# Attention block on one core: the first steps in another order (filler products, weight scaling, sums, maxima)

## The chip, the cores and the metric

One Trainium2 chip, one of its cores. The metric is device microseconds of one execution. A core has five engines that run side by side, each working through its own instructions in order: TensorE (PE in the profile; its weight loads are PEld), VectorE (DVE), ScalarE (ACT), GpSimd (POOL) and SyncE (SP), which here only issues transfers. They wait for one another through semaphores.

## What is computed

A residual attention layer: 64 batches of 128 tokens, 512 features, 16 heads of 64, one key and one value head shared by all (with a null key in front), a bias per head, a causal mask and a mask of keys.

```python
xn = layernorm(x, g_in)
q = (xn @ Wq).reshape(b, n, H, DH).transpose(0, 2, 1, 3) * scale
kv = xn @ Wkv
k, v = (kv[..., :DH], kv[..., DH:])          # the null key and value are put in front
sim = jnp.einsum('bhid,bjd->bhij', q, k) + bias
sim = where(causal or masked, -max, sim)
attn = jax.nn.softmax(sim, axis=-1)
out = jnp.einsum('bhij,bjd->bhid', attn, v)
out = layernorm(out @ Wo, g_out)
return x + out
```

All in float32.

## The kernel before

The kernel is one program whose order is written out by hand: `step(n)` runs for n from -6 to 62 and issues, for several batches at different stages, the pieces of work one after the other. Each engine gets its share of the pieces in just this order. Batches are taken in groups of four (a group g has 512 tokens).

**Tokens.** `norm_stats(m)` takes mean and variance of x_m on DVE and raises the variance to -1/2 on POOL (L246). `norm_apply(m)` scales: on DVE for the first four (L253), later a small product on DVE (nmr, L258) and then ACT (L259). Where one step has two m, both statistics are issued before either scaling. `norm_T(m)` transposes x_m with PE (pxT, L268) and copies it to xT with ACT (L269). From batch 8 on, DVE transposes (L278) and transfers move it.

**Projections.** For group 0, `q_plain` makes eight chunks of q from the weights wq (pq, L373; each has four products, over rows 2, 0, 3, 1 of wq) and ACT copies them to qT (L380). For later groups the same result comes from seven products instead of eight, per pair of halves (`product`, L422; `keep`, ACT L433; `q_out`, DVE L443 or ACT L440). They need sums of weights, s1, s2, s4 (`weight_sums`, DVE L385 to L387) and s3 (`weight_sum_3`, POOL L390, written over the part of wq that only group 0 reads), and four sums of tokens per group (`token_sum`, POOL L404). `kv_mm` (pkv, L308) makes keys, values and the null key's scores in one product; `kv_out` takes it out of PSUM on DVE (ktok L320, vs L324).

**Weights at the start.** g_in is multiplied into the rows of wq by `weights_q` (DVE L844 or ACT L848) and into wkv by DVE (L872). `weights_kv_prod` multiplies wq by the null key on POOL (L864), and DVE sums that (nq, L876) into 16 further columns of wkv (L857). `causal(u)` fills the upper triangle of the bias on POOL (L199); the second half of the bias is loaded after `causal(1)`, since it overwrites rows that this one touches.

**Softmax.** `bias_add` puts bias and mask into a tile S (POOL L466), `null_copy` the null scores (POOL L475), `scores` is PE (ps, L495) and DVE (add, L508), `scores_max` DVE (L513), `exps` ACT, one row at a time with its sum (L522), `rinv` DVE (L539), `scale` POOL (L543). Each is done for hf 0 (64 keys) and hf 1 (128 keys). The probabilities of batches 0 and 1 are transposed on PE (`attn_T_pe`, L610 and L615), those of later ones on DVE (L575) and moved by transfers (L601) into aTb, which starts as zeros.

**Values and output.** `values` and `values_end` multiply by the values (po, L636). Between the halves stands a tiny copy of DVE, `done` (L668), for order; ACT takes the result to oT (L680). Batch 0 goes through `out_mm` (py, L697) and `out_stats`; later ones in pairs with seven products (L750).

**Filler.** `keep_busy(k)` issues k products of the unit matrix with itself that nobody reads (L1191). A product of float32 leaves two records in the trace.

**Transfers.** SP issues nearly all of them in program order, and one queue works them off. Each of its eight semaphores is used in turn, so a transfer also waits until the one eight places ahead of it has landed. `load_second`, `load_late` (wo, gob) and `loads_late` issue the input of the front.

PSUM tiles with the tag "w" have two buffers, which transposes, pkv, pk, po and py share in turn.

Of the kernel before, what the change touches and what calls it, by code (L numbers as in the profile page):

```python
# [8 lines left out]
FP = mybir.dt.float32  # L9
U8 = mybir.dt.uint8  # L10
AF = mybir.ActivationFunctionType
ALU = mybir.AluOpType
# [5 lines left out]
def kernel(  # L18
# [59 lines left out]
    nc = tc.nc  # L78
# [60 lines left out]
    def load_mask(g):  # L139
        m8s[g] = gp.tile([P, TOK], U8, tag="m8", name=f"m8_{g}")  # L140
        nc.sync.dma_start(
            out=m8s[g],
            in_=mask[g * GB : (g + 1) * GB].rearrange("b n -> (b n)").partition_broadcast(P),
        )
# [28 lines left out]
    )  # L173

    def load_second():
        nc.sync.dma_start(out=nbh, in_=null_bias.partition_broadcast(P))
        nc.sync.dma_start(out=nvb, in_=cond[1].partition_broadcast(P))
        load_mask(0)
        for m in (4, 5, 6):
            load_x(m)  # L180
        load_bias(1)
        for r in range(2):
            nc.sync.dma_start(
                out=nv2[r * DH : (r + 1) * DH, :], in_=cond[1].unsqueeze(1)
            )

    def load_bias(u):
        rows = slice(u * DH, (u + 1) * DH)
        bias_r = attn_bias.rearrange("(u f r) i j -> u r i f j", u=2, r=2)[u]
        for r in range(2):  # L190
            rf = slice(r * NF, (r + 1) * NF)
            nc.sync.dma_start(out=biasp[rows, rf, 0:NL], in_=bias_r[r, 0:DH, :, 0:NL])
            nc.sync.dma_start(out=biasp[rows, rf, NL:], in_=bias_r[r, DH:N])
# [193 lines left out]
        nc.vector.tensor_tensor(s4, a12, s2, ALU.subtract)  # L387

    def weight_sum_3():
        nc.gpsimd.tensor_tensor(s3, a11, a21, ALU.subtract)  # L390

    def token_sum(g, k):

        xS[g, k] = gp.tile([P, GB // 2, HK, N], FP, tag=f"xS{k}", name=f"xS{k}_{g}", bufs=1)
        lo, hi = xT[g][:, 0 : GB // 2], xT[g][:, GB // 2 :]
        b11, b12 = lo[:, :, lo_k], hi[:, :, lo_k]
        b21, b22 = lo[:, :, hi_k], hi[:, :, hi_k]
        p, m = {
            1: (b12, b11),
            2: (b22, xS.get((g, 1))),  # L400
            3: (b22, b12),
            4: (b21, xS.get((g, 2))),
        }[k]
        nc.gpsimd.tensor_tensor(xS[g, k], p, m, ALU.subtract)  # L404
# [55 lines left out]
    def bias_add(b):  # L460
        g, t = divmod(b, GB)
        if b in (B3 + 1, B3 + 4):
            S[b] = gp.tile([P, R8, ROW], FP, tag="xT", name=f"s_{b}")
        else:
            S[b] = sp.tile([P, R8, ROW], FP, tag="s", name=f"s_{b}")
        nc.gpsimd.tensor_tensor(  # L466
            S[b][:, :, 1 : ROW - 1],
            biasp,
            mneg[g][:, t].unsqueeze(1).broadcast_to([P, R8, NL + N]),
            ALU.add,  # L470
        )

    def null_copy(b):
        g, t = divmod(b, GB)
        nc.gpsimd.tensor_copy(  # L475
            S[b][:, :, 0 : ROW : ROW - 1],
            nv[g][:, t, DH:].rearrange("p (k e) -> p e k", k=2),
        )
# [38 lines left out]
    def exps(b, hf, lo=0, hi=R8):  # L517
        if hf == 0 and lo == 0:
            rsum[b] = small.tile([P, 2, R8], FP, tag="rsum", name=f"rsum_{b}")
        for k in range(lo, hi):  # L520
            row = S[b][:, k, WITH_NULL[hf]]
            nc.scalar.activation(  # L522
                row,
                row,
                AF.Exp,
                bias=nmax[b][:, hf, k : k + 1],
                accum_out=rsum[b][:, hf, k : k + 1],
            )
# [257 lines left out]
    def pair_pow(b):  # L786
        nc.gpsimd.tensor_tensor(yn[b][1], yn[b][1], nhalf, ALU.pow)
# [23 lines left out]
    def out_stats(b):  # L811
        st = small.tile([P, 6], FP, tag="st", name=f"sto_{b}")
        nc.vector.bn_stats(st, ys[b])
        mv = small.tile([P, 2], FP, tag="mvo", name=f"mvo_{b}")
        nc.vector.bn_aggr(mv, st)
        rstd = small.tile([P, 1], FP, tag="rstdo", name=f"rstdo_{b}")
        nc.vector.tensor_scalar(rstd, mv[:, 1:2], EPS, None, ALU.add)
        nc.gpsimd.tensor_tensor(rstd, rstd, nhalf, ALU.pow)
        y = hp.tile([P, DIM], FP, tag="y", name=f"y_{b}", bufs=3)
        nc.vector.scalar_tensor_tensor(  # L820
            y, ys.pop(b), mv[:, 0:1], gob, ALU.subtract, ALU.mult
        )
        if b == B - 1:

            nc.vector.scalar_tensor_tensor(y, y, rstd, res.pop(b), ALU.mult, ALU.add)
        else:
            yr[b] = y, rstd
        ys[b] = y
# [11 lines left out]


    def weights_q(kc):
        if kc < 2:
            nc.vector.tensor_scalar(  # L844
                wq[:, kc, :], wq[:, kc, :], gin8[:, kc : kc + 1], None, ALU.mult
            )
        else:
            nc.scalar.activation(  # L848
                wq[:, kc, :], wq[:, kc, :], AF.Copy, scale=gin8[:, kc : kc + 1]
            )  # L850
# [9 lines left out]
            )  # L860

    def weights_kv_prod(kc):
        prods[kc] = sp.tile([P, H, DH], FP, tag="s", name=f"prod_{kc}")
        nc.gpsimd.tensor_tensor(  # L864
            prods[kc],
            wq[:, kc, :].rearrange("p (h d) -> p h d", d=DH),
            nkb.unsqueeze(1).broadcast_to([P, H, DH]),
            ALU.mult,
        )
# [9 lines left out]
    def step(n):  # L879
        def ok(b, end=B):  # L880
            return 0 <= b < end
# [33 lines left out]
            null_copy(nb)  # L915
        if third:
            pair_pow(p4)
        for m in mns:
            norm_stats(m)
        if fast and f == 0 and fill:  # L920
            for k in range(1, 5):
                token_sum(qg, k)
            if n == -2:
                weight_sum_3()
        if n == -4:
            bias_add(0)
            bias_add(1)
# [7 lines left out]
        if one:  # L935

            out_mm(n - 1, 0, NF if n > B3 + 1 else NC)
            if n == 1:
                attn_T_pe(1)
                bias_add(nb)  # L940
                null_copy(nb)
                out_stats(0)
        if fast:
            if f == 0:
                q_tile(qg)
# [5 lines left out]
            scores_max(B3 + 1, 0)  # L951
        if last:
            product(last_g, last_f, 4, ps_q, "a", start=False)
        if soft:
            exps(eb, 0, 0, 4)
        if third:
            out_part(p4 + 1, 0, "X")
# [10 lines left out]
        if 2 * GB <= mb < B:  # L968
            tokens_T(mb)
            if (mb + 1) % GB == 0:  # L970
                tokens_out(mb // GB)
        if soft:
            exps(eb, 0, 4)
        if soft and n != B3 + 1:
            rinv(eb, 0)
            scale(eb, 0)
        if third:
# [21 lines left out]
            product(qg, f, 2, ps_w, "w")  # L999
        elif q and not fast:  # L1000
            q_plain(qg, 2 * f)
        if soft:
            exps(eb, 1, 0, 2)
        if third and n != B3:
            pair_norm(p4)
# [19 lines left out]
        elif first:  # L1025
            out_keep("X", "yp1", "p1")
            out_product(p12, 2, ps_w, "w")
            out_part(p12, 0, "w", "yp1")
        if soft:
            exps(eb, 1, 2, 4)  # L1030
        if soft and not second:
            exps(eb, 1, 4, 6)
# [34 lines left out]
                mask_neg(qg)  # L1067
            out_part(p5673, 1, "Y", "yu2")
        if ok(n + 1) and fill:
            exps(n + 1, 1)  # L1070
        if one and n == 1:
            residual(0)
        if n == B3 - 1:
# [2 lines left out]
        if sc and n != B3:  # L1076
            scores(nb, 0)
            scores_add(nb, 0)
            if ok(n + 1) and fill:
                rinv(n + 1, 1)  # L1080
                scale(n + 1, 1)
        split = sc and n != B3
        if n == B3:
            pair_nmr(p4 + 1)
        if ok(n):
            values(n, split)
        if third and n != B3:
            pair_residual(p4 + 1)
            store(p4 + 1)
# [4 lines left out]
        if not ok(n) and fast:  # L1094
            product(qg, f, 6, ps_q, "a", start=False)
            keep("a", "u2")
        if ok(n) and not split:
            values_end(n, split)
            if n > B3 + 1:
                out_mm(n - 1, NF)  # L1100
# [6 lines left out]
            store(p4 + 1)  # L1107
            scores_max(nb, 0)

        late = first and fast  # L1110
        if sc:
            scores(nb, 1)
            scores_add(nb, 1)
# [63 lines left out]
        if n == B2 - 2:  # L1177
            second_aTb()
        if n == -4:
            for m in range(GB - 1):  # L1180
                kv_out(m, kv_mm(m))
                if m:
                    kT_out(m - 1, k_T(m - 1))
# [10 lines left out]
    nc.vector.tensor_scalar(gin8, gin, DH**-0.5, None, ALU.mult)  # L1194
    norm_stats(0)
    norm_stats(1)
    norm_apply(0)
    norm_T(0)
    norm_stats(2)
    norm_apply(1)  # L1200
    norm_T(1)
    norm_stats(3)
    norm_apply(2)
    norm_T(2)
    keep_busy(8)
    norm_apply(3)
    norm_T(3)
    keep_busy(10)
    load_second()
    weights_q(2)  # L1210
    weights_q(0)
    weights_q(3)
    weights_q(1)
    nc.gpsimd.memset(aTb, 0.0)
    for kc in range(2):
        weights_kv_prod(kc)
    nc.vector.tensor_scalar(vnb[:, 0:DH], nvb, -1.0, None, ALU.mult)
    null_order(vnb[:, DH:], nbh)
    causal(1)
    load_bias(0)  # L1220
    for n in range(-6, B - 1):
        step(n)
        if n == -6:
            for kc in range(2):
                weights_kv(kc)
            for kc in range(2, KC):
                weights_kv_prod(kc)
            load_late()
        if n == -5:
            for kc in range(2, KC):  # L1230
                weights_kv(kc)
            causal(0)
            mask_neg(0)
            weight_sums()

    load_res(B - 1)
    store(B - 3)
# [47 lines left out]
```

## Time and profile before

| | us |
|---|---|
| three runs | 1125.67, 1126.27, 1128.89 |
| median | 1126.27 |
| profiled execution, time | 1131.23 |
| its span, first to last instruction | 1129.4 |
| PE busy | 1089.5 (96%) |
| DVE busy | 808.0 (72%) |
| POOL busy | 745.3 (66%) |
| ACT busy | 678.1 (60%) |
| matmul pa L422, mean of one record | 0.38 |

The profiled execution is one of its own and stands 5 us above the median. "Busy" is time in which an engine has an instruction in it; since products overlap, a busy PE isn't one at its peak. Times inside the execution count from the span's start. A row of the timeline gives start and length, the engine, the line, what is written and read with its shape, and in brackets the idle time of the engine before it with whatever ended that.

The kernel runs in three stretches: the front up to about 130 us, a long even part, and an end of some 30 us.

### The profile page before, as it was taken

The page shows a single profiled execution, that of the slowest core. Times are in us where ns is not written, and L with a number is a line of the kernel's source. Part 1 is how long each engine was busy: PE and PEld are TensorE (multiplying, and loading weights), DVE is VectorE, ACT ScalarE, POOL GpSimd, SP SyncE. Part 2 cuts the span into 40 slices and gives each one's busy share as a digit, 9 for nine tenths or more (in the row PEclk, how much of TensorE's full clock was granted, in tenths as well). Part 3 has the DMA queues.
Part 4 walks back from the last instruction along what each step waited for, and adds up shares of the span by engine and source line. Part 5 has one row for each costly group of instructions (what it writes and reads, how often), then busy time and mean ns, then how long its engine had stood idle before and what let it go on. Part 6 is the DMA issues. An engine that isn't in the chain of part 4 may idle for free.

```text
span 1129.4 us, 27505 instructions
## 1 busy us (share of the span) xinstructions
PE 1089.5 (96%) x9780; PEld 873.0 (77%) x9780; DVE 808.0 (72%) x1741; ACT 678.1 (60%) x2710; POOL 745.3 (66%) x588
## 2 busy tenths in 40 slices
PE   6988999999999999999999999999999999999987
PEld 4565788888888888788888888888888888888643
DVE  6564677777787777678777768877777886666852
ACT  2345656666765666676565667566566756657651
POOL 5454877767675776767577676757768575777832
PEclk9999999999999999999999999999999999999999
DMA  6313244363454436345343533534353353422333
GB/s 186 121 33 96 63 128 115 93 168 98 128 131 127 118 91 169 98 124 133 122 123 91 165 105 120 132 120 118 100 163 104 125 134 99 114 75 76 96 104 101
DMA packets 107864, 130.09 MB, mean 115 GB/s; under 512 B 29264, under 2 KB 72528, under 8 KB 105936
## 3 DMA queue, kind: packets, MB, share of 16 engines
q1 hardware_dynamic: 106480, 126.96, 40.0%
q8 instruction: 78, 1.28, 0.5%
q10 hardware_dynamic: 1248, 1.38, 0.4%
q14 instruction: 58, 0.48, 0.1%
HBM read 54.86 MB, written 31.46 MB: 76 GB/s over the span
## 4 chain that ended last, share of the span: by engine, by line
PE 68%; DMA 8%; POOL 7%; DVE 6%; SPq 5%; issue 3%; ACT 3%; POOLq 0%; ACTq 0%; DVEq 0%
PE pa L422 14%; PE pyX L750 13%; PE pc L422 7%; PE ps L495 7%; PE po L636 6%; PE pyY L750 6%; DMA x<-in_x_dram 6%; PE pk L308 4%; SPq L601 4%; PE pw L422 3%; PE pyw L750 3%; PE py L697 3%; ACT s L522 2%; POOL s L543 1%; POOL xS L404 1%
## 5 line engine op out<-in xcount | busy, mean ns | idle before, releaser
L522 ACT ACTIVATE s<-s,nmax 128x65 f32<-128x65 f32 (+1 forms) x1024 | 372.2, 368 | 0.4
L466 POOL TENSOR_TENSOR s<-biasp,mneg 128x1536 f32<-128x1536 f32 x64 | 221.1, 3455 | 110.0 <-DVE sb L575 99.0
L543 POOL TENSOR_TENSOR s<-s,rinv 128x512 f32<-128x512 f32 (+1 forms) x128 | 189.2, 1479 | 119.5 <-DVE nmro L794 86.8
L680 ACT ACTIVATE oT<-po,nv 128x512 f32<-128x512 f32 x128 | 81.0, 683 | 203.2 <-PE po L636 203.2
L522 ACT ACTIVATION_READ_ACCUMULATOR s<-s,nmax 128x1 f32 x1024 | 195.2, 191 | 0.0
L750 PE MATMUL pyX<-wT,oT 128*128 128x256 f32 x696 | 164.7, 379 | 0.5 <-DVE kyu L762 0.5
L750 PEld LDWEIGHTS pyX<-wT,oT 128*128 128x128 f32 x696 | 131.9, 190 | 19.4 <-DVE kyu L762 0.9
L508 DVE TENSOR_TENSOR s<-ps,s 128x512 f32<-128x512 f32 (+1 forms) x128 | 121.6, 950 | 14.2 <-PE ps L495 13.3
L495 PEld LDWEIGHTS ps<-kT,qT 64*64 64x64 f32 x4096 | 92.2, 134 | 46.8 <-DVE s L508 24.9
L422 PE MATMUL pa<-xS,wq 128*128 128x256 f32 x480 | 123.7, 380 | 2.0 <-POOL wq L390 1.0
L513 DVE TENSOR_REDUCE nmax<-s 128x8 f32<-128x520 f32 (+1 forms) x128 | 120.2, 939 | 5.1 <-POOL s L475 3.7
L495 PE MATMUL ps<-kT,qT 64*64 64x64 f32 (+1 forms) x4096 | 116.6, 251 | 3.3 <-DVE s L508 2.6
L575 DVE STREAM_TRANSPOSE sb<-s 128x1536 f32<-128x1536 f32 x62 | 110.0, 1774 | 11.6 <-POOL s L543 4.6
L636 PE MATMUL po<-aTb,vs 64*64 64x256 f32 (+1 forms) x1240 | 114.2, 380 | 2.2 <-DVE done L668 2.2
L433 ACT COPY ku<-pa 128x256 f32<-128x256 f32 x120 | 44.7, 372 | 94.4 <-PE pa L422 94.4
L422 PEld LDWEIGHTS pa<-xS,wq 128*128 128x128 f32 x480 | 86.7, 190 | 12.2 <-ACT ku L433 1.6
L308 PE MATMUL pk<-wkv,xT 128*128 128x144 f32 x488 | 70.2, 287 | 0.0
L422 PE MATMUL pc<-xS,wS 128*128 128x256 f32 x240 | 63.2, 386 | 6.9 <-POOL xS L404 6.9
L422 PE MATMUL pa<-xS,wS 128*128 128x256 f32 x240 | 68.8, 409 | 0.0
L443 DVE TENSOR_TENSOR qT<-pw,kp 128x256 f32<-128x256 f32 x60 | 25.4, 424 | 59.8 <-ACT kp L433 59.7
L636 PEld LDWEIGHTS po<-aTb,vs 64*64 64x64 f32 (+1 forms) x1240 | 55.9, 134 | 12.2 <-issue 3.8
L246 POOL TENSOR_TENSOR rstd<-rstd,nhalf 128x1 f32<-128x1 f32 x64 | 35.8, 559 | 44.5 <-DVE rstd L245 44.4
(120 smaller groups left out, 2105.9 us busy)
## 6 DMA issues: line engine op xcount, KB each, us to landing
aTb<-sb SPq DMA_DIRECT2D x369, 64.0 KB
x<-in_x_dram SPq DMA_DIRECT2D x64, 256.0 KB
res<-in_x_dram SPq DMA_DIRECT2D x64, 256.0 KB
out_dram<-y SPq DMA_DIRECT2D x64, 256.0 KB
aTb<-sb SPq DMA_DIRECT2D x492, 32.0 KB
xd<-xb SPq DMA_DIRECT2D x14, 1024.0 KB
xT<-xd SPq DMA_DIRECT2D x56, 256.0 KB
wo<-in_L_cond_Wo_dram SPq DMA_DIRECT2D x1, 2048.0 KB
```

Of the source, the lines that this page charges most:

```text
L308: nc.tensor.matmul(pkv, xT[g][:, t, kc, :], wkv[:, kc, :], start=(kc == 0), stop=(kc == KC - 1),)
L422: nc.tensor.matmul(prod[tag], w[:, kc, f * P : (f + 1) * P], t[:, :, kc, :], start=(start and kc == 0), stop=(kc == HK - 1), skip_group_ch ...
L466: nc.gpsimd.tensor_tensor(S[b][:, :, 1 : ROW - 1], biasp, mneg[g][:, t].unsqueeze(1).broadcast_to([P, R8, NL + N]), ALU.add,)
L495: nc.tensor.matmul(pv[u * DH : (u + 1) * DH, r, f, :], qT[g][rows, f, t, hf, u], kT[b][rows, 0:nk], start=True, stop=True,)
L508: nc.vector.tensor_tensor(sv, pss.pop((b, hf)), sv, ALU.add)
L513: nc.vector.tensor_reduce(nmax[b][:, hf], S[b][:, :, WITH_NULL[hf]], AX.X, ALU.max, negate=True)
L522: nc.scalar.activation(row, row, AF.Exp, bias=nmax[b][:, hf, k : k + 1], accum_out=rsum[b][:, hf, k : k + 1],)
L543: nc.gpsimd.tensor_tensor(sv, sv, rinvs.pop((b, hf)).unsqueeze(2).broadcast_to([P, R8, sv.shape[2]]), ALU.mult,)
L575: nc.vector.transpose(sb.rearrange("p j e q -> p e j q"), S[b][:, :, 1 : ROW - 1].rearrange("p e (j k) -> p e j k", k=Q),)
L636: nc.tensor.matmul(pos[b][u][r * DH : (r + 1) * DH, half], vals[keys, b % GB, 0:DH], aT_of(b)[keys, slots, r * NF : (r + 1) * NF], start=s ...
L680: nc.scalar.activation(oT[b][:, u * NF : (u + 1) * NF, :].rearrange("p f (s q) -> p s f q", q=Q), po[u].rearrange("p h i f q -> p (h i) f q"),
L750: nc.tensor.matmul(prod[key], h[:, c, :], w[:, c, :], start=(start and c == 0), stop=(c == HC - 1), skip_group_check=not start,)
```

## The change

It edits the front only.

- The unread products: before, eight between the third and the fourth transposes and ten after the fourth; after, 5, 4, 2, 2 and 3, ahead of, between and behind the four.
- wq: rows 0 and 1 on DVE, 2 and 3 on ACT before; rows 2, 0 and 3 on DVE and only row 1 on ACT after.
- `weights_kv_prod`: the four come one after the other on POOL, in four tiles instead of two in turn, with the power of x_4 after the first; the fill of the bias comes after them.
- The memset of aTb moves from the start into step -4, the null value's preparation (vnb) from the start to the end of step -5.
- In SP's order x_4 to x_6 and the first half of the bias come before the mask and the null values; the second half of the bias is issued after mask 1 and x_7.
- `weight_sums` moves from the end of step -5 to step -4, ahead of the evacuation of pkv. `weight_sum_3` goes from POOL to DVE and, with the token sums, ahead of the statistics of its step.
- The maxima of hf 1 in the steps below 0 come after `q_out`.
- Step -1: two exponentials of hf 1, then a copy (ku), then the other six. Step 0: the reciprocals and the scaling of batch 1 come after `values`. Step 1: all exponentials of hf 0, their scaling and four of hf 1 come ahead of the bias addition and of `out_stats`.

```diff
--- before.py
+++ after.py
@@ -173,12 +173,12 @@
     )

     def load_second():
-        nc.sync.dma_start(out=nbh, in_=null_bias.partition_broadcast(P))
-        nc.sync.dma_start(out=nvb, in_=cond[1].partition_broadcast(P))
-        load_mask(0)
         for m in (4, 5, 6):
             load_x(m)
         load_bias(1)
+        load_mask(0)
+        nc.sync.dma_start(out=nbh, in_=null_bias.partition_broadcast(P))
+        nc.sync.dma_start(out=nvb, in_=cond[1].partition_broadcast(P))
         for r in range(2):
             nc.sync.dma_start(
                 out=nv2[r * DH : (r + 1) * DH, :], in_=cond[1].unsqueeze(1)
@@ -387,7 +387,7 @@
         nc.vector.tensor_tensor(s4, a12, s2, ALU.subtract)

     def weight_sum_3():
-        nc.gpsimd.tensor_tensor(s3, a11, a21, ALU.subtract)
+        nc.vector.tensor_tensor(s3, a11, a21, ALU.subtract)

     def token_sum(g, k):

@@ -840,7 +840,7 @@


     def weights_q(kc):
-        if kc < 2:
+        if kc != 1:
             nc.vector.tensor_scalar(
                 wq[:, kc, :], wq[:, kc, :], gin8[:, kc : kc + 1], None, ALU.mult
             )
@@ -860,7 +860,10 @@
             )

     def weights_kv_prod(kc):
-        prods[kc] = sp.tile([P, H, DH], FP, tag="s", name=f"prod_{kc}")
+
+        pool, tag = ((sp, "s"), (sp, "s"), (hp, "sb"), (hp, "xb"))[kc]
+        bufs = None if kc < 2 else 1
+        prods[kc] = pool.tile([P, H, DH], FP, tag=tag, name=f"prod_{kc}", bufs=bufs)
         nc.gpsimd.tensor_tensor(
             prods[kc],
             wq[:, kc, :].rearrange("p (h d) -> p h d", d=DH),
@@ -915,13 +918,13 @@
             null_copy(nb)
         if third:
             pair_pow(p4)
+        if fast and f == 0 and fill:
+            if n == -2:
+                weight_sum_3()
+            for k in range(1, 5):
+                token_sum(qg, k)
         for m in mns:
             norm_stats(m)
-        if fast and f == 0 and fill:
-            for k in range(1, 5):
-                token_sum(qg, k)
-            if n == -2:
-                weight_sum_3()
         if n == -4:
             bias_add(0)
             bias_add(1)
@@ -937,9 +940,6 @@
             out_mm(n - 1, 0, NF if n > B3 + 1 else NC)
             if n == 1:
                 attn_T_pe(1)
-                bias_add(nb)
-                null_copy(nb)
-                out_stats(0)
         if fast:
             if f == 0:
                 q_tile(qg)
@@ -951,7 +951,15 @@
             scores_max(B3 + 1, 0)
         if last:
             product(last_g, last_f, 4, ps_q, "a", start=False)
-        if soft:
+        if n == 1:
+            exps(eb, 0)
+            rinv(eb, 0)
+            scale(eb, 0)
+            exps(eb, 1, 0, 4)
+            bias_add(nb)
+            null_copy(nb)
+            out_stats(0)
+        elif soft:
             exps(eb, 0, 0, 4)
         if third:
             out_part(p4 + 1, 0, "X")
@@ -969,9 +977,9 @@
             tokens_T(mb)
             if (mb + 1) % GB == 0:
                 tokens_out(mb // GB)
-        if soft:
+        if soft and n != 1:
             exps(eb, 0, 4)
-        if soft and n != B3 + 1:
+        if soft and n not in (1, B3 + 1):
             rinv(eb, 0)
             scale(eb, 0)
         if third:
@@ -999,7 +1007,7 @@
             product(qg, f, 2, ps_w, "w")
         elif q and not fast:
             q_plain(qg, 2 * f)
-        if soft:
+        if soft and n != 1:
             exps(eb, 1, 0, 2)
         if third and n != B3:
             pair_norm(p4)
@@ -1026,7 +1034,7 @@
             out_keep("X", "yp1", "p1")
             out_product(p12, 2, ps_w, "w")
             out_part(p12, 0, "w", "yp1")
-        if soft:
+        if soft and n != 1:
             exps(eb, 1, 2, 4)
         if soft and not second:
             exps(eb, 1, 4, 6)
@@ -1067,7 +1075,7 @@
                 mask_neg(qg)
             out_part(p5673, 1, "Y", "yu2")
         if ok(n + 1) and fill:
-            exps(n + 1, 1)
+            exps(n + 1, 1, 0, R8 if n == 0 else 2)
         if one and n == 1:
             residual(0)
         if n == B3 - 1:
@@ -1076,14 +1084,14 @@
         if sc and n != B3:
             scores(nb, 0)
             scores_add(nb, 0)
-            if ok(n + 1) and fill:
-                rinv(n + 1, 1)
-                scale(n + 1, 1)
         split = sc and n != B3
         if n == B3:
             pair_nmr(p4 + 1)
         if ok(n):
             values(n, split)
+        if n == 0:
+            rinv(1, 1)
+            scale(1, 1)
         if third and n != B3:
             pair_residual(p4 + 1)
             store(p4 + 1)
@@ -1094,6 +1102,10 @@
         if not ok(n) and fast:
             product(qg, f, 6, ps_q, "a", start=False)
             keep("a", "u2")
+        if n == -1:
+            exps(0, 1, 2)
+            rinv(0, 1)
+            scale(0, 1)
         if ok(n) and not split:
             values_end(n, split)
             if n > B3 + 1:
@@ -1107,7 +1119,7 @@
             store(p4 + 1)
             scores_max(nb, 0)

-        late = first and fast
+        late = fast and (first or n < 0)
         if sc:
             scores(nb, 1)
             scores_add(nb, 1)
@@ -1177,6 +1189,7 @@
         if n == B2 - 2:
             second_aTb()
         if n == -4:
+            weight_sums()
             for m in range(GB - 1):
                 kv_out(m, kv_mm(m))
                 if m:
@@ -1194,44 +1207,46 @@
     nc.vector.tensor_scalar(gin8, gin, DH**-0.5, None, ALU.mult)
     norm_stats(0)
     norm_stats(1)
+    keep_busy(5)
     norm_apply(0)
     norm_T(0)
     norm_stats(2)
+    keep_busy(4)
     norm_apply(1)
     norm_T(1)
     norm_stats(3)
+    keep_busy(2)
     norm_apply(2)
     norm_T(2)
-    keep_busy(8)
+    keep_busy(2)
     norm_apply(3)
     norm_T(3)
-    keep_busy(10)
+    keep_busy(3)
     load_second()
     weights_q(2)
     weights_q(0)
     weights_q(3)
     weights_q(1)
-    nc.gpsimd.memset(aTb, 0.0)
-    for kc in range(2):
-        weights_kv_prod(kc)
-    nc.vector.tensor_scalar(vnb[:, 0:DH], nvb, -1.0, None, ALU.mult)
-    null_order(vnb[:, DH:], nbh)
-    causal(1)
-    load_bias(0)
+    weights_kv_prod(0)
     for n in range(-6, B - 1):
         step(n)
         if n == -6:
+            for kc in range(1, KC):
+                weights_kv_prod(kc)
+            causal(1)
+            load_bias(0)
             for kc in range(2):
                 weights_kv(kc)
-            for kc in range(2, KC):
-                weights_kv_prod(kc)
             load_late()
         if n == -5:
             for kc in range(2, KC):
                 weights_kv(kc)
             causal(0)
             mask_neg(0)
-            weight_sums()
+            nc.vector.tensor_scalar(vnb[:, 0:DH], nvb, -1.0, None, ALU.mult)
+            null_order(vnb[:, DH:], nbh)
+        if n == -4:
+            nc.gpsimd.memset(aTb, 0.0)

     load_res(B - 1)
     store(B - 3)
```

## The prediction

> **What bounds the kernel.** I read the page first (span 1129.4 us, TensorE busy 96%, granted clock 0.9 or more in all 40 slices), then a table of busy time by stage, then the timeline of the first 130 us. In the stages below the columns are: stage, length, busy us of PE, PEld, DVE, ACT and POOL with their counts, granted clock, DMA share, GB/s.
>
> ```profile
> 0.00:10.00 10.00, 1.30 (x5) 0.90 (x6) 4.21 (x13) 2.07 (x3) 4.01 (x11) 1.00 0.74 269
> 10.00:20.00 10.00, 9.37 (x51) 8.34 (x51) 8.02 (x11) 3.84 (x5) 7.40 (x5) 1.00 0.71 201
> ...
> 40.00:50.00 10.00, 7.41 (x35) 5.76 (x35) 4.26 (x18) 2.99 (x6) 7.89 (x4) 0.83 0.08 26
> 50.00:60.00 10.00, 8.72 (x34) 5.09 (x32) 4.59 (x16) 4.13 (x9) 2.27 (x4) 1.00 0.22 54
> 60.00:70.00 10.00, 7.95 (x93) 6.07 (x93) 3.77 (x5) 1.71 (x5) 6.78 (x6) 1.00 0.12 42
> ...
> 110.00:120.00 10.00, 7.66 (x109) 5.12 (x101) 6.31 (x10) 7.34 (x29) 6.18 (x4) 1.00 0.05 14
> 120.00:130.00 10.00, 8.44 (x74) 6.97 (x78) 4.62 (x17) 6.77 (x32) 8.49 (x7) 1.00 0.30 84
> ...
> 200.00:1100.00 900.00, 890.17 (x8252) 732.43 (x8251) 673.23 (x1442) 574.57 (x2340) 615.12 (x480) 1.00 0.42 117
> ```
>
> From 130 us on PE is 99% busy and nothing there is edited, so whatever the front gains or loses by then arrives whole at the end. Up to 130 us PE idles 8.7 us before 10, and 13 us between 40 and 130. In 10 to 20 part of the "busy" is filler: the unread products. The timeline names the waits (start, length, engine, line, instruction; in brackets the idle time before it and what ended it):
>
> ```profile
> 11.86 1.58 DVE L253 TENSOR_SCALAR x<-x,mv,rstd 128x512 f32<-128x512 f32 x1 [0.44 <-POOL rstd L246]
> ...
> 18.77 7.03 PE L373 MATMUL pq<-xT,wq 128*128 128x512 f32 x16
> ...
> 42.60 0.66 PE L268 MATMUL pxT<-ident,x 128*128 128x128 f32 x4 [2.18 <-ACT x L259]
> ...
> 60.65 1.13 PE L422 MATMUL pc<-xS,wS 128*128 128x256 f32 x4 [1.93 <-POOL xS L404]
> ...
> 66.76 1.13 PE L422 MATMUL pa<-xS,wq 128*128 128x256 f32 x4 [1.01 <-POOL wq L390]
> ...
> 91.20 0.96 PE L636 MATMUL po<-aTb,vs 64*64 64x256 f32 x8 [2.17 <-DVE done L668]
> ...
> 112.53 0.43 PE L636 MATMUL po<-aTb,nv 64*64 64x256 f32 x2 [1.64 <-DVE qT L443]
> ```
>
> The first shows a second fact: the same normalisation took 0.54 us three times and 1.58 us here, while POOL's memset of aTb ran from 11.77 to 13.15. DVE was shut out until POOL had finished.
>
> **Start of the projections: -4.1 us.** Before, 16 records (eight unread products) run from 12.44 to 16.06 and hold back the fourth transposes, whose x was ready at 13.44; the copy to xT ends at 17.32, ACT scales wq rows 2 and 3 at 1.14 each, ten more products run, and pq starts at 18.77. After, the memset is gone from this place, so x_3 is ready at 12.4. Two products (4 records of 3.62/16 = 0.23) stand before its transposes: third transposes end 12.3, products 13.2, transposes (0.85 while slow, as at 15.86) 14.0, ACT's copy (0.58) 14.6, three products beside it. DVE scales rows 2, 0, 3 in 0.74 each from 12.4 to 14.6; ACT's row 1 (1.14) is done at 15.8 and needed only as the fourth product, at 14.6 + 3 x 0.87. So pq starts at about 14.6 (14.0 to 15.2).
>
> **The products for the null key: +1.2.** POOL now does prod 0 (2.8, as the first before), the power (0.55), then prods 1, 2, 3 (2.35 each) and only then the causal fill (0.66 + 1.09): 13.9 to about 26.4, against 22.83 before. DVE's small scalings and copies beside them are shut out: wkv's scaling, 0.28 alone, took 2.42 at 25.10 beside a prod. So nq 0 and 1 end late, x_5's statistics near 28, its power after the fill, ACT's 0.81 ends at 29.8, where PE wants it at 14.6 + 6.9 + 0.35 + 6.9 = 28.75. That stall is new, about 1.2. The three extra tiles remove POOL's waits for nq (3.1 us), which is why it reaches the fill in one run.
>
> **The transfer of x_8 eats the rest of that gain.** The second half of the bias waits for the fill; on SP's queue wo, gob and x_8 stand behind it:
>
> ```profile
> 26.68 0.43 SPq L210 DMA_DIRECT2D wo<-in_L_cond_Wo_dram  x1
> 27.16 0.58 SPq L211 DMA_DIRECT2D gob<-in_L_cond_g_out_dram  x1
> 33.61 0.67 SPq L120 DMA_DIRECT2D x<-in_x_dram  x1
> ...
> 37.00:38.00 1.00, 1.00 (x3) 0.39 (x3) 0.97 (x2) 0.59 (x1) 0.00 (x0) 1.00 0.32 104
> 38.00:39.00 1.00, 1.00 (x4) 0.41 (x3) 0.97 (x2) 0.00 (x0) 0.00 (x0) 1.00 0.20 74
> ```
>
> The last bytes of these land near 39.3 (the last two lines are one-us stages), just before x_8's statistics at 40.48. After, wo is issued at about 26.4 + 3 x 0.65 = 28.4, 1.7 later, with x_7's 256 KB (0.65 us at the 400 GB/s seen from 31 to 36) no longer between: x_8 lands near 40.3. DVE takes the statistics of x_6 and x_8 before the scale of either, so PE's transposes of x_6 stand at about 42.4 (before: 42.60), although the sums s1, s2, s4 (3 x 1.22) no longer precede them. If transfers pass each other, x_8 is there at 34 and the transposes at 37.2: 5 us better. I take the late one; nbh, 8 KB issued at 8.13 behind 3 MB, landed at 16.03. Masks and null values, moved behind the bias on SP, are wanted only at 31 us or later and cost nothing.
>
> **The sums on VectorE: +0.3 or +8.** They now stand between the scale of x_8 and ktok, that is, at the moment when POOL begins its two bias additions (3.43 each, 42.17 before). Here a row and a rule part. The row: DVE's TENSOR_TENSOR of 128x1024 at L508 takes 1212 ns on average over 64 executions beside a POOL that is busy 66% of the time; no TENSOR_TENSOR of DVE in this trace is ever stretched. But all of those have one input in PSUM. s1, s2, s4 have both in SBUF, and ran (1221, 1224, 1224) with POOL idle. The Trainium skill, "SBUF — State Buffer", section "SBUF: two separate sides", says that a VectorE instruction with two SBUF inputs competes for a port pair with a GpSimd instruction that reads SBUF, and that the loser is blocked for the winner's whole length; this speaks against the change. By the row: the sums end at x_8 + 5.7 instead of ktok starting at x_8 + 4.2, but pkv's second product, slow after the gap, ends only at + 6.0, and DVE then needs what it needed before: +0.3. By the rule: s1 waits for the first bias addition (to + 5.15), s2 for the second (to + 9.85), ktok starts at + 12.3, pq 6 at + 14.9 instead of + 7.95: +7, and after a gap of that length the clock is low for a while (0.5 from 44 to 47 after a gap of 2.18), +1.5. I take the row, which is of the same opcode, size and type, with little margin; the other end is a rival.
>
> **Token sums and s3: -2.5.** POOL's four token sums (1.27) now come before x_10's statistics: they start with the copy of x_7's transposes, 8.2 us after pq 6, instead of 10.9. s3 goes from POOL (2.36) to DVE (1.22). So pc's wait of 1.93 and pa's of 1.01 go, and qT before the last maximum removes 0.75 (at 70.36). DVE's order lets PE keep 0.9 of it only as slack: next late is ACT's chain of exponentials for batch 0, which starts when the qT copy allows. Its first two, then ku, then six remove 0.43, but the transposes of batch 0 still wait for the scale. Net at those transposes: 2.5.
>
> **Step 0: -3.0.** rinv and scale of batch 1 go behind `done`; the 2.17 before 91.20 goes, and with it the low clock of 92 to 94 (pa 2.07 for 1.03, pk 1.48 for 1.15, together 1.3, of which I count 0.8). The scale is needed only after py (6.9 us), which hides it.
>
> **Step 1: -2.0.** Twelve exponentials now fill ACT's idle 8.98 us behind py, so kp no longer waits for them, and the 1.64 before 112.53 and half of the later 0.74 go. bias_add (3.45 on POOL) moves behind the scale, with DVE waiting nowhere else for it.
>
> The memset of aTb (1.38) lies before x_7's power, needed 5 us later: nothing. A further +1.0 is for slow clock in the longer gap before x_6.
>
> **Sum.** -4.1 + 1.2 + 2.7 (x_8) + 0.3 + 1.0 - 2.5 - 3.0 - 2.0 = -6.4. The profiled execution took 1131.23 (span 1129.4 and 1.8 around it), 5.0 above the median 1126.27; it would give 1124.8. On the median: **1119.9 us**.
>
> **Rivals.** Measurements of this kernel tell about 0.3% (3.4 us) from no change.
> - *The port pair blocks the sums* (34%): place DVE's s1 and s2, price 8.5 instead of 0.3, giving 1126.27 + 1.8 = 1128.1, slower. For it: the rule, and the stretched rows of DVE at 11.86 and 25.10. Against: those are one-input forms. It decides once the blocking exceeds 6.4. The later gains could be 2 more or 3 less: 1126 to 1131.
> - *x_8 is early* (15%): -5 more, 1115, down to 1113. For it: x_8 is issued 3 us earlier than before. Against: nbh above.
> - *The later waits are hidden anyway* (13%): ACT's exponentials hold steps 0 and 1 at their former distance, only the -2.5 and 1 of step 0 remain: 1123.8. For it: ACT is 75% busy in 70 to 80. Against: PE waits in 91.20 and 112.53 are for order on DVE, not for ACT's amount.
> - The forecast keeps 38%, 1117 to 1123.
>
> **Chances.** Faster: 0.36 of the forecast, 0.15, 0.06 of the third, 0.02 of the blocked case: 0.59. Same: 0.02 + 0.11 + 0.06 = 0.19. Slower: 0.21 + 0.01 = 0.22. Range 1113 to 1130: it takes in the early x_8 and most of the blocked case.
>
> **What would show it.** pq starting near 14.6; a PE wait before the transposes of x_5; DVE waiting for x_8's transfer near 34 to 40; s1, s2 at 1.22 each (forecast) or near 4 (rival); pc and pa near 60 without waits; `done` without 2.17; no wait before po of batch 1. A longer idle time between x_6's transposes and pq 6 than the 1.3 us of before proves me wrong, as does a PE gap anywhere after 130 us.

## The result and the profile after

The changed kernel is slower: ratio 1.0071 to the kernel before, 95% interval [1.0054, 1.0088]; medians of five runs each 1135.91 and 1128.89 us. Forecast were 6.4 us less; by the ratio 8.0 more came (0.71% of 1129; the two medians lie 7.0 apart). The profiled execution took 1135.35 (span 1133.6) against 1131.23. The median of the same kernel before drifts from one set of runs to the next (1126 to 1131), so kernels are compared by their ratio to the runs of before in their own set; 0.1% is 1.1 us.

The timeline of the changed kernel, same columns as before, at the place that the prediction called decisive:

```profile
41.64 0.69 DVE L241 BATCH_NORM_STATS2 st<-x 128x6 f32<-128x512 f32 x1 [7.19 <-DMA x<-in_x_dram]
...
43.33 7.81 POOL L466 TENSOR_TENSOR s<-biasp,mneg 128x1536 f32<-128x1536 f32 x2
...
43.53 4.33 DVE L385 TENSOR_TENSOR wS<-wq 128x1024 f32<-128x1024 f32 x1
43.76 1.11 PE L268 MATMUL pxT<-ident,x 128*128 128x128 f32 x4 [6.17 <-ACT x L259]
...
47.89 4.33 DVE L386 TENSOR_TENSOR wS<-wS,wq 128x1024 f32<-128x1024 f32 x1
51.08 1.38 POOL L1249 MEMSET aTb<- 128x1536 f32 x1
52.26 1.23 DVE L387 TENSOR_TENSOR wS<-wq,wS 128x1024 f32<-128x1024 f32 x1
53.40 0.28 DVE L320 COPY ktok<-pkv 128x128 f32<-128x128 f32 x1
...
53.98 0.45 PE L342 MATMUL pkT<-ident,ktok 128*128 128x128 f32 x1 [5.61 <-DVE vs L324]
```

Read it upwards from the last line. PE idles 5.61 us because ktok has not been copied out of PSUM. ktok stands in DVE's order behind s1, s2 and s4 (L385 to L387), and s1 and s2 take 4.33 us each where they took 1.22 before; s4, with the additions over, takes 1.23. Beside them POOL's two bias additions run from 43.33 to 51.1. DVE has no idle time in these rows: an instruction that is shut out, that is, started but held up, counts as busy. A second gap of 6.17 stands before it: the first row shows DVE waiting 7.19 for x_8. pq of step -4 begins at 56.59 instead of 48.43. The clock falls too; the table of stages (stage, length, busy time of the five engines, granted clock, DMA share, GB/s) has 0.66 twice where it had 0.83 and 1.00:

```profile
40.00:50.00 10.00, 4.61 (x20) 4.39 (x20) 7.72 (x7) 2.60 (x4) 7.18 (x3) 0.66 0.11 34
50.00:60.00 10.00, 6.02 (x17) 3.97 (x18) 7.53 (x18) 0.42 (x2) 3.52 (x4) 0.66 0.04 7
```

Later, from the same timeline:

```profile
66.50 1.42 DVE L390 TENSOR_TENSOR wq<-wq 128x1024 f32<-128x1024 f32 x1
66.92 2.14 POOL L404 TENSOR_TENSOR xS<-xT,xS 128x512 f32<-128x512 f32 x1
...
71.46 0.55 POOL L246 TENSOR_TENSOR rstd<-rstd,nhalf 128x1 f32<-128x1 f32 x1
72.04 0.21 DVE L258 TENSOR_SCALAR nmr<-mv,rstd 128x1 f32<-128x1 f32 x1 [2.19 <-POOL rstd L246]
72.91 1.10 PE L495 MATMUL ps<-kT,qT 64*64 64x128 f32 x32 [2.67 <-DVE s L508]
...
88.31 1.51 PE L610 MATMUL paU<-ident,s 128*128 128x128 f32 x8 [2.30 <-POOL s L543]
...
101.54 0.33 PE L342 MATMUL pk<-ident,ktok 128*128 128x128 f32 x1 [0.99 <-ACT oT L680]
```

Two rows of the kernel before, to compare with the one at 88.31:

```profile
77.78 1.13 PE L422 MATMUL pa<-xS,wq 128*128 128x256 f32 x4 [0.43 <-ACT ku L433]
...
79.81 1.09 PE L610 MATMUL paU<-ident,s 128*128 128x128 f32 x8 [0.90 <-POOL s L543]
```

The waits of pc (1.93) and pa (1.01) are gone as forecast, but the power of x_10 (71.46) now stands behind all four token sums; DVE's nmr waits for it, the addition to the scores stands behind nmr, and PE waits 2.67. s3, now on DVE, and the second token sum get in each other's way as the sums and the bias additions do: the token sum takes 2.14 instead of 1.27, which makes that power 0.87 later still. Where PE waited 0.43 for ku and 0.90 for the scale of batch 0, it waits 2.30 in one piece, and paU, the transposes of batch 0's probabilities, is slow after it (1.51 for 1.09). In step 0 the wait of 2.17 before po is gone, but a new one of 0.99 stands before pk: ACT copies oT at 100.82, behind the eight exponentials of batch 1, although the last product of po ends at 99.5.

### The profile page after: what moved, and what is told of

It is laid out like the page before. It is cut to its first block, busy times and chain, and to the rows that moved or that the text cites. A ratio compares the mean times of both kernels' runs of the same rounds, so it can differ in the third digit from the quotient of the medians.

```text
span 1133.6 us, 27497 instructions
## 1 busy us (share of the span) xinstructions
PE 1089.3 (96%) x9776; PEld 874.3 (77%) x9776; DVE 815.7 (72%) x1743; ACT 677.0 (60%) x2709; POOL 745.1 (66%) x587
## 4 chain that ended last, share of the span: by engine, by line
PE 73%; DMA 7%; DVE 5%; POOL 5%; SPq 5%; issue 3%; ACT 2%; POOLq 0%; DVEq 0%; ACTq 0%
PE pa L422 15%; PE pyX L750 14%; PE pc L422 7%; PE ps L495 7%; PE pyY L750 7%; PE po L636 7%; DMA x<-in_x_dram 6%; PE pk L308 4%; SPq L601 4%; PE pw L422 3%; PE pyw L750 3%; PE py L697 2%; PE pq L373 2%; POOL xS L404 1%; ACT s L522 1%
## 5 line engine op out<-in xcount | busy, mean ns | idle before, releaser
L308 PEld LDWEIGHTS pk<-wkv,xT 128*128 128x128 f32 x488 | 63.5, 191 | 0.1
```

Of the source, the lines that this page charges most:

```text
L308: nc.tensor.matmul(pkv, xT[g][:, t, kc, :], wkv[:, kc, :], start=(kc == 0), stop=(kc == KC - 1),)
```

## The experiments

Theory A: POOL's bias additions shut the sums out. Rival B: x_8's late transfer is what costs, and the sums only fill a wait that is there anyway. Rival C: the later edits give nothing or cost.

**1. The sums alone put back**, before x_6's statistics:

```diff
         if n == -4:
-            weight_sums()
             for m in range(GB - 1):
...
             null_order(vnb[:, DH:], nbh)
+            weight_sums()
         if n == -4:
```

> The changed kernel with one edit undone: s1, s2, s4 go back to the end of step -5, ahead of x_6's statistics. Theory A (VectorE's sums of two SBUF tensors are shut out for the length of POOL's bias additions): VectorE has nothing to do from 34.5 to 41.6 us while it waits for x_8, so the sums now run there at 1.22 each and cost nothing; ktok starts near 46 instead of 53.4, pq of step -4 near 49.7 instead of 56.6, and the whole kernel takes about 1128 to 1129 (7 less than the changed kernel, ratio to the kernel before about 1.000). Theory B (what costs is x_8's late transfer behind wo, the sums only fill a wait that is there anyway): pq of step -4 moves by less than 2 us, 1134 to 1136 (ratio 1.006).

Measured: 1.0004 [0.9995, 1.0013]; pq of step -4 at 48.35. The sums take 1.22 each while DVE would wait for x_8. Undoing this one edit returns 0.67%, 7.6 us. B alone is out: it expected 1.006.

**2. wo and gob later**, so that x_8 is not behind them:

```diff
                 weights_kv(kc)
-            load_late()
...
             nc.gpsimd.memset(aTb, 0.0)
+            load_late()
```

> The changed kernel with the loads of wo and gob issued after step -4 instead of after step -6, so that x_8 stands behind neither. Both theories: x_8's statistics start near 34.5 instead of 41.6, and x_6's transposes follow the last product of step -5 at about 37.6 without the 6.2 us of idle. Theory A: the sums are then shut out just as long (4.3 each for s1 and s2), ktok starts about 11.8 after x_8's statistics, pq of step -4 near 49.5: 7 less than the changed kernel, about 1129. Theory B: pq of step -4 near 43.5, 13 less, about 1123.

Measured: 1.0007 [0.9996, 1.0017]. The timeline of this kernel:

```profile
35.19 0.69 DVE L241 BATCH_NORM_STATS2 st<-x 128x6 f32<-128x512 f32 x1 [1.92 <-DMA x<-in_x_dram]
36.88 7.81 POOL L466 TENSOR_TENSOR s<-biasp,mneg 128x1536 f32<-128x1536 f32 x2
37.08 4.33 DVE L385 TENSOR_TENSOR wS<-wq 128x1024 f32<-128x1024 f32 x1
...
41.44 4.33 DVE L386 TENSOR_TENSOR wS<-wS,wq 128x1024 f32<-128x1024 f32 x1
...
47.53 0.45 PE L342 MATMUL pkT<-ident,ktok 128*128 128x128 f32 x1 [7.21 <-DVE vs L324]
```

x_8 is there 6.4 us earlier, and everything behind it moves by as much, with the 4.33 unchanged (pq of step -4 at 50.14): PE's idle time is now nearly all in one piece, 7.21. So two delays are in series, x_8 first and the shut-out behind it.

**3. Both edits together.**

> The changed kernel with both edits: the sums at the end of step -5, wo and gob after step -4. Theory A: nothing stands in the way of ktok any more, TensorE is the bound: x_6's transposes at 37.6, pq of step -4 near 43.5, 13 less than the changed kernel: about 1122.5, faster than the kernel before (ratio 0.995). Theory B: the same as with wo and gob alone, within 1 us, about 1123. Theory C (the front only moves a wait; what later steps wait for, ACT and POOL, takes the gain back): 1127 to 1130, with new waits of TensorE between 60 and 90.

Measured: 0.9947 [0.9931, 0.9963], pq of step -4 at 43.31. With x_8 early the sums are worth 0.60%, with x_8 late 0.67%: the two add, as A says.

**4. POOL's work moved instead of DVE's:** the bias additions ahead of the statistics, the sums where the change put them.

```diff
+        if n == -4:
+            bias_add(0)
+            bias_add(1)
         for m in mns:
             norm_stats(m)
...
-        if n == -4:
-            bias_add(0)
-            bias_add(1)
```

> The changed kernel with POOL's two bias additions emitted ahead of the statistics of x_6 and x_8 instead of behind them; the sums stay where the change put them, behind x_8's statistics and scale factors. Theory A: POOL runs the additions in its idle time from 33.4 to 40.3, is free when the sums start near 43.5, and s1, s2, s4 take 1.22 each; ktok near 47.5, pq of step -4 near 50, 6.5 less than the changed kernel: about 1129.5. If the sums are slow for another reason (their place, the clock, the DMA traffic), they stay at 4.3 each and the time stays within 1 us of 1136.

Measured: 0.9989 [0.9979, 0.9998]. The timeline of this kernel:

```profile
32.00 6.81 POOL L466 TENSOR_TENSOR s<-biasp,mneg 128x1536 f32<-128x1536 f32 x2 [0.78 <-DVE mneg L452]
...
42.29 1.38 POOL L1249 MEMSET aTb<- 128x1536 f32 x1
...
42.51 1.22 DVE L385 TENSOR_TENSOR wS<-wq 128x1024 f32<-128x1024 f32 x1
43.76 1.23 DVE L386 TENSOR_TENSOR wS<-wS,wq 128x1024 f32<-128x1024 f32 x1
45.02 1.22 DVE L387 TENSOR_TENSOR wS<-wq,wS 128x1024 f32<-128x1024 f32 x1
```

The sums are the same, in the same place of DVE's order, and x_8 is still late (40.62); only the bias additions are gone from beside them, and the sums take 1.22 each. This is the cleanest test of A. POOL's memset runs beside s1 here and does not slow it.

**5. The kernel before with this part alone.**

```diff
             mask_neg(0)
-            weight_sums()
...
         if n == -4:
+            weight_sums()
             for m in range(GB - 1):
```

> The kernel before with one part of the change alone: s1, s2, s4 moved from the end of step -5 to step -4, behind x_8's scale factors and beside POOL's bias additions. Theory A (blocked by POOL): x_8's statistics come a little earlier than 40.48 us, as the sums no longer precede them, about 39.4; s1 and s2 take 4.3 each, ktok near 51.5 instead of 44.7, pq of step -4 near 54.5 instead of 48.4; 6 to 7 more, about 1.006 times the kernel before. By the row of the prediction (the sums at 1.22 each): pq of step -4 within 0.5 us of 48.4 and a ratio of 1.000.

Measured: 1.0058 [1.0045, 1.0072], pq of step -4 at 55.06:

```profile
41.81 7.80 POOL L466 TENSOR_TENSOR s<-biasp,mneg 128x1536 f32<-128x1536 f32 x2
42.00 4.33 DVE L385 TENSOR_TENSOR wS<-wq 128x1024 f32<-128x1024 f32 x1
46.37 4.33 DVE L386 TENSOR_TENSOR wS<-wS,wq 128x1024 f32<-128x1024 f32 x1
```

Moved alone, the sums cost 6.6 us, without any other part of the change.

**6. The sums back, and token sums and s3 as before.** The two places of the diff that touch them are undone, nothing else:

```diff
-        nc.vector.tensor_tensor(s3, a11, a21, ALU.subtract)
+        nc.gpsimd.tensor_tensor(s3, a11, a21, ALU.subtract)
...
         for m in mns:
             norm_stats(m)
+        if fast and f == 0 and fill:
+            for k in range(1, 5):
+                token_sum(qg, k)
+            if n == -2:
+                weight_sum_3()
```

> The changed kernel with the sums back at the end of step -5, and the token sums behind x_10's statistics and s3 on POOL as before. By the prediction's term (-2.5 for this edit) it takes 2.5 us more than the kernel with the sums alone put back, a ratio to the kernel before of about 1.0026. By the reading of the traces the edit trades the waits before pc (1.9) and pa (1.0) for one of 2.7 before the second half of batch 0's scores, where POOL's power of x_10 now stands behind four token sums, and is worth 0.5 at most: ratio 1.000 to 1.001, with the transposes of batch 0's weights within 1 us of 79.3.

Measured: 0.9980 [0.9970, 0.9991]. Both expectations missed: without this edit the kernel is 0.24%, 2.7 us, faster than in experiment 1. How much of it is the token sums' and how much s3's was not separated.

**7. The sums back, and the steps -1, 0 and 1 as before** (the places of the diff from `n == 1` down to `late`).

> The changed kernel with the sums back at the end of step -5, and the order of exponentials, scales and maxima in the steps -1, 0 and 1 as before. By the prediction's terms (-3.0 and -2.0) it takes 5 us more than the kernel with the sums alone put back, a ratio of about 1.0048, with 2.2 of idle before po of step 0 and 1.6 before that of step 1. By the traces so far (the stretch from pc of step 0 to py 2.8 shorter, from pc of step 1 to pk 2.2 shorter, the next 0.6 longer) 4.4 more, 1.0043. If ACT's amount of exponentials hides the gain (the third rival), 1 us more or less: 1.000 to 1.001.

Measured: 1.0015 [1.0003, 1.0026], 1.2 us more than in experiment 1, not 5: close to what was expected by the third rival, ACT's exponentials hiding the gain, but only in part for its reason. In the profiled executions, from pc of step 0 to py it takes 1.2 longer than in experiment 1: the wait of 2.18 before po is back, and the 0.99 for oT is gone. From pc of step 1 to pk it takes 3.4 longer, 1.3 of which is a low clock behind the wait of 1.64 that another execution with the same wait (that of before) does not have; from there to the next pc it takes 1.5 less. And from pk of step -2 to pc of step 0 it takes 1.8 less, which is no matter of ACT's amount. The timeline of this kernel shows why:

```profile
77.74 1.13 PE L422 MATMUL pa<-xS,wq 128*128 128x256 f32 x4 [1.25 <-ACT ku L433]
...
79.77 1.09 PE L610 MATMUL paU<-ident,s 128*128 128x128 f32 x8 [0.90 <-POOL s L543]
```

There are two waits, 2.15 together, and no slow clock behind them; the change makes one wait of them. This is the same in every trace here: from paU to pc of step 0 it takes 5.66 us in the five traces in which the wait before paU is 0.90 (before, experiments 5, 7, 9 and 11), and 7.17 to 7.26 in the eight in which it is 2.00 to 2.47.

**8. A version meant to beat both:** wo and gob late; the sums in step -3, where POOL is idle; the power of x_10 ahead of the fourth token sum.

```diff
+            for k in range(1, 4):
+                token_sum(qg, k)
         for m in mns:
             norm_stats(m)
+        if fast and f == 0 and fill:
+            token_sum(qg, 4)
...
             norm_apply(m)
+        if n == -3:
+            weight_sums()
```

> The changed kernel with wo and gob loaded after step -4, the sums in step -3 behind the scale factors of x_7 and x_9, where POOL is idle from about 46 to 50, and the fourth token sum behind x_10's statistics. Theory A: the sums take 1.22 each; x_6's transposes at 37.3 instead of the 38.5 of the kernel with the sums ahead of x_6's statistics, pq of step -4 near 42.3, the wait before the second half of batch 0's scores 1.5 instead of 2.7: about 2.2 less than that kernel, ratio to the kernel before about 0.993. If something else of step -3 waits for the sums, 0.995 or more.

Measured: 0.9909 [0.9892, 0.9926], 0.002 below what was expected; pq of step -4 at 42.13, the wait before the scores 1.45. Which of its two new edits gives how much of the 0.4% against experiment 3 was not separated.

**9. The same with step -1's exponentials as before the change** (eight together, then reciprocal and scale).

> The kernel with the sums in step -3, wo and gob late and the token sums parted (ratio 0.991 to the kernel before), with the order of step -1's exponentials of batch 0 as it was before the change: all eight of the second half together, then reciprocal and scale. Theory: the change's order turns two waits of TensorE (1.25 for ku and 0.90 for the scale) into one of 2.29, about as long, but only the long one is followed by a low clock (paU 1.5 for 1.09, the stretch from paU to pc of step 0 7.2 for 5.7). With the waits parted again that stretch takes 5.7, and the whole 1.8 less: ratio about 0.989. If the low clock comes anyway, or ku's wait returns at full length beside it, the same or 0.4 more: 0.991 to 0.9915.

Measured: 0.9896 [0.9875, 0.9917]: the fastest, 11.7 us below the kernel before, but not apart from experiment 8 (the intervals overlap). Its timeline:

```profile
46.68 1.22 DVE L385 TENSOR_TENSOR wS<-wq 128x1024 f32<-128x1024 f32 x1
...
56.67 1.10 PE L495 MATMUL ps<-kT,qT 64*64 64x128 f32 x32 [1.45 <-DVE s L508]
...
69.77 1.13 PE L422 MATMUL pa<-xS,wq 128*128 128x256 f32 x4 [0.86 <-ACT ku L433]
71.80 1.09 PE L610 MATMUL paU<-ident,s 128*128 128x128 f32 x8 [0.90 <-POOL s L543]
```

The waits are parted (0.86 and 0.90) and the transposes take 1.09; the stretch from paU to pc of step 0 takes 5.66, not the 7.17 of experiment 8.

**10. The kernel of experiment 1, profiled a second time.**

> A second look at the changed kernel with the sums at the end of step -5, as its first profiled execution (1127.5) was 3 less than the median of its 22 runs (1130.5). If the medians lose their 3 us to the granted clock, this look shows, at equal waits, one more stretch of low clock than the first (which had 0.71 in 40 to 50 and 0.84 in 80 to 90), most likely behind the wait of 2.67 before the second half of batch 0's scores, which the order of the token sums brings; a time near 1130. If it is something else, a new wait of TensorE of about 3 us stands somewhere.

Measured: 1131.34, 3.9 more than the first profiled execution (1127.48).

```profile
65.06 1.62 PE L495 MATMUL ps<-kT,qT 64*64 64x128 f32 x32 [2.67 <-DVE s L508]
...
82.07 1.54 PE L610 MATMUL paU<-ident,s 128*128 128x128 f32 x8 [2.30 <-POOL s L543]
```

The waits are those of the first execution, but this time the clock is low behind the 2.67 too (granted clock 0.83 in 60 to 70, where the first had 1.00). The scores take 1.62 instead of 1.10, and the stretch from pk of step -2 to the next pc 7.20 instead of 6.12. Another 1.2 had come by pq of step -4 (49.50): x_6's transposes are 0.4 later, and the clock is lower there as well (0.66 for 0.71 in 40 to 50). The last 1.1 comes behind 130 us. So the same program has the low clock behind the same wait in one execution and not in another.

**11. The first part alone** (experiment 6 with the steps of experiment 7 undone too).

> The kernel before with the first part of the change alone: unread products among the first transposes, the weights scaled mostly by VectorE, the products for the null key in one run, the new order of loads; sums, token sums, s3 and the steps -1 to 1 as before. By the prediction's terms (-4.1 for the start of the projections, +1.2 for the products, +2.7 for x_8, +1.0 for the clock) 0.8 more than before, ratio 1.0007, pq of step -4 within 1 us of the 48.4 of before. By the differences of the runs so far (with the token sums +1.7, with the steps -2.3, with both +0.5) -1.1, ratio 0.999. If the front really arrives 3 us earlier at the end, 0.9975.

Measured: 0.9996 [0.9986, 1.0006]. pq begins at 14.27 instead of 18.77, and pq of step -4 at 49.88 instead of 48.43 (expected within 1 us of it); PE waits 6.59 before x_6's transposes instead of 2.18, for x_8.

## Why the prediction was wrong

The parts, each against its term in the prediction:

| part | term, us | measured, us | from |
|---|---|---|---|
| front, with x_8 and the clock | -4.1 +1.2 +2.7 +1.0 = +0.8 | -0.5 | experiment 11 |
| s1, s2, s4 on DVE | +0.3 (or +7 +1.5) | +7.6; alone +6.6 | 1; 5 |
| token sums and s3 | -2.5 | +2.7; +2.1 | 1 less 6; 7 less 11 |
| steps -1, 0, 1 | -5.0 | -1.2; -1.8 | 1 less 7; 6 less 11 |

With the first of each pair they make +8.6, and +8.0 was measured. A difference of two experiments is uncertain by 1.5 to 2.2 us, the front by 1.1, so only the sums stand far clear of it; the -1.2 is not told from nothing. The rows are cut by edits, not quite by the prediction's terms: its -2.5 also counted the maxima and the exponentials of step -1, which are undone in experiment 7, not in 6.

**The step that failed** is the choice "I take the row, which is of the same opcode, size and type, with little margin". The row had one input in PSUM; the sums have both in SBUF, and the rule of the Trainium skill ("SBUF — State Buffer", section "SBUF: two separate sides") is for just these. The trace of before held no DVE instruction with two SBUF inputs beside a POOL that reads SBUF, so the row could say nothing, and the prediction had named this difference itself. In its place came the shut-out: 4.33 for s1 and for s2, +7.6 us where +0.3 stood. The rival's working by the rule was right in kind and close in size: its price of 8.5 was measured as 7.6, and pq of step -4, which it put at x_8 + 14.9, came at 56.59 - 41.64 = 14.95. That the last figure is met so exactly is luck: ktok came at + 11.8 instead of + 12.3, and from ktok to pq it took 3.2 instead of 2.6. The sign that the prediction had named for being wrong came too, PE's idle time between x_6's transposes and pq: 5.61, where the profile of before has 0.41 (not the 1.3 that the prediction gives).

**But the rival's sum, +1.8, was also 6 us too low**, for two terms that both cases shared. *Token sums and s3*: the prediction counted the waits that go and did not follow POOL's queue behind them; x_10's power, with DVE's nmr and the scores behind it, was late next. In the traces the new wait costs about what the old ones did: from pq of step -4 to paU it takes 31.63 without the edit (experiment 6), 30.94 with it (experiment 1), and 32.57 with the low clock behind the wait (experiment 10). The rest of the loss goes with the clock. The granted clock, averaged over the timed runs, is 0.9912 with this edit and 0.9940 without it (experiments 1 and 6), 0.9914 and 0.9933 in the other pair (7 and 11). If time went fully with it, these 0.0028 and 0.0019 of 1130 us would be 3.2 and 2.1 us, the whole loss; by the runs of experiments 1, 6 and 7 among themselves, where 0.001 goes with 0.7 us, they are 2.0 and 1.3. Experiment 10 shows one such execution; that the others lose their time in the same place is inferred from the averages, not shown.

*Steps -1, 0 and 1*: the 2.17 and the 1.64 went, and in the profiled pair the stretches of steps 0 and 1 are 2.8 and 2.2 us shorter, 0.6 of it given back (forecast -3.0 and -2.0). Step 1 thus came near its term. But of the 2.8, 1.6 was chance: from pc of step 0 to py the profile of before has 10.88 us, with the low clock of 92 to 94, experiment 7 at the same wait of 2.18 has 9.26, and the changed kernel 8.07. At equal clock step 0 is worth 1.2, since the 2.18 goes and the 0.99 for oT comes. That is the third rival's figure, and for its reason: the prediction had set aside ACT's amount ("PE waits in 91.20 and 112.53 are for order on DVE, not for ACT's amount"), and ACT's exponentials are what oT stands behind. Step -1 was costed at next to nothing ("remove 0.43") and gave a wait in one piece with the low clock behind it, 1.5 in the stretch after it. Rival C of the experiments thus holds for the token sums and for step -1, and only in part for step 0.

**What was right:** the transfer of x_8 (41.6, forecast 40.3) eats the gain of the front; experiment 2 shows that it is wo and gob that hold it back, since with these behind it x_8 is there at 35.19. Whether they do so by their place in the queue or by sharing the DMA engines with x_8 is not told apart. The stall of 1.2 before x_5's transposes did not come: in the changed kernel its scaling ended just in time, and where pq began near 14, from the second pq to the third it takes 7.4 (experiment 1) and 7.6 (experiment 11) against 7.3 before. x_3 took 0.55, as forecast for a front without the memset. pq began at 15.84 instead of 14.6, as x_1 landed late in that execution; experiment 11 has 14.27.

What stays open: how the low clock picks its executions, and which of token sums and s3 costs more.

## What to carry to other kernels

When an instruction moves to another engine or another place, look at where its operands lie, not only at its opcode and size: a row of the trace vouches only for the same memories beside the same neighbour. The cure is a stretch in which the neighbour is idle (experiments 1, 4 and 8). Where a wait goes, walk along the queue of every engine that was reordered to what is late next. Parting a wait can be worth more than shortening it: before paU the low clock followed each gap of 2.0 us or more, and did not follow two gaps of 2.15 together.

## What the runs showed of the hardware

- DVE's sum or difference of two SBUF tensors (128x1024, 1.22 us alone) and POOL's addition of two SBUF tensors exclude each other: 4.33 beside a bias addition of 3.4, in all three kernels that have them side by side (the changed one, experiments 2 and 5); POOL pays as well, two bias additions taking 7.8 instead of 6.8 us, and a token sum 2.14 instead of 1.27 beside s3.
- POOL's memset does not shut such a sum out (1.22 at 42.51 in experiment 4, the memset from 42.29 to 43.67), though in the kernel before the same memset stretched DVE's one-input scaling from 0.54 to 1.58. The Trainium skill ("SBUF — State Buffer", section "Who interferes with whom") says this of two-input instructions, that they contend with a GpSimd instruction that reads SBUF and not with one that only writes it; experiment 4 agrees.
- Low clock behind a gap of TensorE of about 2 us comes in some executions and not in others: behind the 2.67 before the scores in two of seven traces, behind the 2.17 before po of step 0 in two of four, behind the 1.93 before pc in one of four; but behind the 2.00 to 2.47 before paU in eight of eight, and behind 0.90 there in none of five. It costs 1.1 to 1.6 us each time. What makes the difference is not shown.
